# A state-space block and a mixture of experts in one kernel: five weight splits moved ahead of the first slots, and the second block's front begun five slots later

## The chip, the cores and the metric

The kernel runs on one NeuronCore of a Trainium2 chip. It takes float32 inputs and gives float32 outputs. The metric is the device time of one execution in microseconds; the time of a kernel is the median of its runs. All engines named here belong to that one core: TensorE (PE in the profile, with its weight loads as PEld), VectorE (DVE), ScalarE (ACT), GpSimd (POOL), and SyncE (SP), which only issues DMAs here. ScalarE's queue issues a few DMAs at the start and the end.

## The reference: what is computed

The input `u` has 16 batches of 512 tokens with 128 features. Each batch passes through two residual halves, both with a layer norm before and after:

```python
x = x + layernorm(state_space(layernorm(x)))      # Bu = x B^T; convolution with 64 complex modes; y = h C^T + D x
x = x + layernorm(experts(layernorm(x)))
```

The convolution kernel is `exp(t * log(eig))`, with eigenvalues on the unit circle that are worked out from `a_params`. The second half is a dense mixture of 8 experts: every token goes through every expert.

```python
h   = silu(x @ w_gate[e]) * (x @ w_up[e])          # 128 -> 512
out = sum over e of (h @ w_down[e]) * cw[:, e]     # 512 -> 128
cw  = softmax(x @ w_router) * softmax((x @ w_gating) / 0.1), normalised over e
```

## The kernel before

**Blocks and slots.** A block is one batch: 512 tokens. The expert half of block b is cut into 32 slots, one for each of 8 experts and 4 quarters of the 512 hidden features, so slot n has b = n // 32, e = n // 4 % 8, and there are 512 slots. In a slot, `up` (L554) makes g and uu, 128 hidden features by 512 tokens each; `gate` (L569) multiplies silu(g) and uu; `down` (L589) adds the slot's share to the expert's output d four slots later (`LAG`).

**Three matmuls for one.** A float32 product is made of float32r parts: each operand has a high part (a cast) and a low part (what the cast lost), and `mm3` (L337) issues high by high (L338), low weight by high (L339) and high weight by low (L340). A full slot is thus 9 matmuls of 128x512. The parts of the hidden h are `hi` (L580, ScalarE) and `lo` (L586, on VectorE, or on POOL where the planner's list `lo_pool` says so). The 24 weight matrices (3 for each expert: gate, up, down, in that order, numbered k = 3e + j) are split too: a cast on ScalarE (L110) and a subtraction on POOL (L115). The first `AHEAD` = 3 weights are split before slot 0 by `rest` (L679): TensorE multiplies by the identity and subtracts the high part by a negated identity, each of these in float32 with two passes, and ScalarE writes the result (L684). The others are split in the slots, one at a time (L837 to L839).

**Engines take their instructions in the order in which the program issues them.** The order is written out by hand in the loop over slots (L807 to L846), and a small planner decides where the rest goes. In slot n the loop issues: `hi` of slot n-1; g, uu and silu (`sg`, L564) of slot n; `down` of slot n-4; then, every fourth slot, `combine` (L596), which multiplies a finished d by the token weights `cwb` of its expert (L601 for the first expert of a block, L606 for the others) and adds it up; then one weight split; then `steps`; then `lo` of slot n-1; then the gate of slot n. For `combine` of expert e of block b that is slot 32b + 4e + 9.

**The planner.** `chain(b)` (L615) is a generator: layer norm, state space and second layer norm of block b (`front`, L346), then `route(b)` (L408), which makes the token weights. Each `yield` gives the slots to wait and the time it needs on VectorE, ScalarE and POOL. `steps` (L794) runs those that are due and fit into `SLOT` + a margin; a chain with `hurry` 1 may take two steps in a slot and waits a slot less. Block 1's chain begins in slot 0 with hurry 1 (L821), the others at max(4, 32b - 67). `back(b)` (L467) is the last layer norm of a finished block: a transpose on VectorE (`ob`, L473), four DMA writes (`sco`, L476), a DMA back (`ot`, L481), then statistics.

**From the logits to `cwb`.** `route` makes the logits on TensorE (`lg`, L415), the powers on POOL (`ez`, L433, eight instructions; block 0 uses ScalarE's exponential instead), sums and quotients on VectorE (L436 to L446), then the transpose `cwT` (L451). SP writes `cwT` to DRAM in four DMAs (`scw`, L454) and reads it back for two experts at a time, broadcast to all partitions (`cwb`, L462, 512 KB each). SP issues its DMAs in order, each after its own waits.

**Before slot 0.** Block 0's state space runs in a hand-ordered stretch (L641 to L773) with two halves of 256 tokens. `yp` (L675, L698) is its output, `residual` (L726) makes x2 and its statistics, `rstd` (L497) the scale on POOL (L505), `norm` (L513) the normalised xn, TensorE transposes it (L752), ScalarE writes the high part xh and the plain copy (L755, L756), VectorE the low part xl (L757). `keep_warm` (L734) issues 9 and 4 matmuls whose result nobody reads.

**Buffers that matter.** g has two PSUM banks, uu three, d two; `sg` two tiles in SBUF, `hi` and `lo` five each. The first `OWN` = 8 weights are loaded into tiles of `hi` and `lo`, the later ones into five tiles of their own.

Of the kernel before, what the change touches and what calls it, by code (L numbers as in the profile page):

```python
# [11 lines left out]
F32 = mybir.dt.float32  # L12
# [7 lines left out]
P = 128  # L20
T = 512
NT = T // P
# [4 lines left out]
NF = F // P  # L27
LAG = 4
LEAD = 67
OWN = 8  # L30
WARM = 9, 4, 0
AHEAD = 3
LN_EPS = 1e-5


# [12 lines left out]
def sandwich(ctx, tc, x, a_params, B_w, C_w, Dv, w_router, w_gating, w_gate, w_up, w_down, sines, out):  # L48
# [31 lines left out]
            nc.sync.dma_start(out=xts[b][:, k], in_=x[b].rearrange("(c p) d -> p c d", p=P)[:, k])  # L80


    spare = [hp.tile([P, F], F32R, name=f"spare{i}", tag="lo", bufs=LAG + 1).bitcast(F32) for i in range(2)]

# [49 lines left out]
    dbc = const.tile([P, D], F32, name="dbc")  # L136
    for k in range(AHEAD, OWN):
        load_w(k)
        if k == 4 and NB > 1:
            load_x(1)  # L140
            nc.sync.dma_start(out=dbc, in_=Dv.partition_broadcast(P))

# [25 lines left out]
    def bank(pl, tag, name):  # L168
        return pl.tile([P, T], F32, name=name, tag=tag)
# [176 lines left out]
    def front(b):  # L346
# [58 lines left out]
        vec.tensor_tensor(xl, xT, xh.bitcast(F32), ALU.subtract)  # L405
        blocks[b] = dict(xh=xh, xl=xl, x2=x2, xT=xT)

    def route(b):  # L408

        G2 = NT * 2  # L410
        xT = blocks[b]["xT"]
        yield 1, 0, 0, 0, "f"
        lg = ps_f.tile([P, G2, E], F32, name=f"lg{b}", tag="f")
        for c in range(NT):
            pe.matmul(  # L415
                lg[:, 2 * c : 2 * c + 2], xT[:, P * c : P * c + P], wrg.rearrange("d g e -> d (g e)"),
                start=True, stop=True,
            )
        yield 1, 0.4, 0, 0
        bc = lambda t, n: t.unsqueeze(2).broadcast_to([P, n, E])  # L420
        mx = small.tile([P, G2], F32, name="mx", bufs=2)
        vec.tensor_reduce(mx, lg, AX.X, ALU.max)
        ez = small.tile([P, G2, E], F32, name="ez", bufs=2)
        vec.tensor_tensor(ez, lg, bc(mx, G2), ALU.subtract)
        own[0] = False
        if b == 0:
            e4 = ez.rearrange("p (c g) e -> p c g e", g=2)
            act.activation(e4[:, :, 0], e4[:, :, 0], AF.Exp)
            act.activation(e4[:, :, 1], e4[:, :, 1], AF.Exp, scale=10.0)
        else:  # L430
            for i in range(G2):
                yield 1, 0, 0, 1.62
                gp.tensor_tensor(ez[:, i], bases.rearrange("p c g e -> p (c g) e")[:, i], ez[:, i], ALU.pow)  # L433
        yield 2, 0.65, 0, 0
        sm = small.tile([P, G2], F32, name="sm", bufs=2)
        vec.tensor_reduce(sm, ez, AX.X, ALU.add)  # L436
        vec.reciprocal(sm, sm)
        vec.tensor_tensor(ez, ez, bc(sm, G2), ALU.mult)
        yield 1, 0.75, 0, 0
        pr = ez.rearrange("p (c g) e -> p c g e", g=2)  # L440
        cw0 = small.tile([P, NT, E], F32, name="cw0", bufs=2)
        vec.tensor_tensor(cw0, pr[:, :, 0], pr[:, :, 1], ALU.mult)
        cs = small.tile([P, NT], F32, name="cs", bufs=2)
        vec.tensor_reduce(cs, cw0, AX.X, ALU.add)
        vec.tensor_scalar(cs, cs, 1e-9, None, ALU.add)
        vec.reciprocal(cs, cs)  # L446
        yield max(1, 32 * b - 8 - now[0]), 0.45, 0, 0
        cwt = cwp[b % 2]
        vec.tensor_tensor(cwt[:, :, 0:E], cw0, bc(cs, NT), ALU.mult)
        cwT = small.tile([P, NT, 32], F32, name="cwT", bufs=2)  # L450
        vec.transpose(cwT, cwt)  # L451
        scw = dram.tile([E, 4, P], F32, name=f"scw{b}", tag="scw")
        for c in range(4):
            nc.sync.dma_start(  # L454
                out=scw.rearrange("e q (c i) -> e q c i", i=32)[:, :, c], in_=cwT[32 * c : 32 * c + E]
            )
        cwb = []
        blocks[b]["cwb"] = cwb
        for i in range(4):
            yield max(1, 32 * b + 8 * i + 2 - now[0]), 0, 0, 0  # L460
            t = fe.tile([P, 2, T], F32, name=f"cwb{b}_{i}", tag="cwb", bufs=3)
            nc.sync.dma_start(  # L462
                out=t, in_=scw[2 * i : 2 * i + 2].rearrange("e q m -> e (q m)").partition_broadcast(P)
            )
            cwb.append(t)
# [47 lines left out]
    def norm(outs, views, rs, nm, shared):  # L513
        act.activation(outs[0], views[0], AF.Identity, scale=rs[:, 0:1], bias=nm[:, 0:1])
        if shared:
            vec.tensor_scalar(outs[1], views[1], rs[:, 1:2], nm[:, 1:2], ALU.mult, ALU.add)
        else:
            act.activation(outs[1], views[1], AF.Identity, scale=rs[:, 1:2], bias=nm[:, 1:2])

    def halves(t):  # L520
        return [[t[:, 2 * h], t[:, 2 * h + 1]] for h in range(2)]
# [110 lines left out]
    def turn(k):  # L632
        for _ in range(k):
            next(rot, None)
# [3 lines left out]
    def stat(c, view):  # L638
        vec.bn_stats(s6s[c // 2][:, c % 2], view)
# [39 lines left out]
    def rest(k, pl, tag):  # L679
        hi, lo = parts(k)  # L680
        ps = bank(pl, tag, f"rest{k}")
        pe.matmul(ps, ident, raw[k], start=True, stop=False)
        pe.matmul(ps, negid[:, 0], hi.bitcast(F32), start=False, stop=True)
        return lambda: act.copy(lo, ps)  # L684
# [10 lines left out]
    def state(c):  # L695
        k = quarter[c]
        vec.tensor_tensor(vm[:, k], v[:, k], tre[:, k], ALU.mult)
        pe.matmul(yps[c], vm[:, k], cT, start=False, stop=True)  # L698

    vec.tensor_tensor(v[:, left], bus[0], tre[:, left], ALU.mult)  # L700
    turn(2)
    scan(left, 0.0)
    turn(2)
    state(0)
    state(1)
    turn(2)
    vec.tensor_tensor(v[:, right], bus[1], tre[:, right], ALU.mult)
    lo0 = rest(0, ps_u, "u")
    lo0()
    scan(right, v[:, 2 * P - 1 : 2 * P])  # L710
    stat(0, yps[0])
    stat(1, yps[1])
    state(2)
    state(3)
    rest(1, ps_g, "g")()
    r0 = rstd(s6s[0])
    stat(2, yps[2])
    stat(3, yps[3])
    r1 = rstd(s6s[1])
    rest(2, ps_f, "f")()  # L720

# [5 lines left out]
            vec.scalar_tensor_tensor(x2[:, c], yps[c], rs[:, i : i + 1], xt[:, c], ALU.mult, ALU.add)  # L729
            stat(c, x2[:, c])  # L730

    warm = bank(ps_g, "g", "warm")

    def keep_warm(k):  # L734
        for _ in range(k):
            pe.matmul(warm, W[0, 0][0][:, :P], W[0, 0][0], start=True, stop=True)

    keep_warm(WARM[0])
    residual(0, r0[1])
    q0 = rstd(s6s[0])  # L740
    residual(1, r1[1])
# [3 lines left out]
    xh = fe.tile([D, T], F32R, name="xh0", tag="xh", bufs=2)  # L745
    xl = fe.tile([D, T], F32R, name="xl0", tag="xl", bufs=2)
    xT = work("ft_x0")
    for h, q in enumerate((q0, q1)):
        norm(halves(xn)[h], halves(x2)[h], q[1], shift(*q), True)
        ps = bank(ps_u, "u", f"xT0{h}")[:, : 2 * P]  # L750
        for i in range(2):
            pe.transpose(ps[:, P * i : P * i + P], xn[:, 2 * h + i], ident)  # L752
        keep_warm(WARM[1 + h])
        k = slice(2 * P * h, 2 * P * h + 2 * P)
        act.copy(xh[:, k], ps)  # L755
        act.copy(xT[:, k], ps)  # L756
        vec.tensor_tensor(xl[:, k], ps, xh[:, k].bitcast(F32), ALU.subtract)  # L757
    for h, r in enumerate((r0, r1)):
        vec.scalar_tensor_tensor(x2m[:, 2 * h : 2 * h + 2], r[0][:, :, 0], -1.0, r[1], ALU.mult, ALU.mult)
    blocks[0] = dict(xh=xh, xl=xl, x2=x2, xT=xT, x2m=x2m)  # L760
    first_route = route(0)

    def first():
# [43 lines left out]
    for n in range(total + LAG):  # L807
        b, s = divmod(n, 32)
        now[0] = n
        busy = [max(0.0, t - SLOT) for t in busy]  # L810
        if n < total:
            take((0.6, 1.0, 0), (9, 9, 9))
        if 0 <= n - 1 < total:
            take((0, 0, 1.23) if lo_pool[n - 1] else (0.6, 0, 0), (9, 9, 9))
            split_hi(n - 1)
        if n < total:
            up(n, *[first] * (n == 0))
        if n == 0:
            begin(n, 0, first_route, 1, routed)
            if NB > 1:  # L820
                begin(n, 1, chain(1), 1)  # L821
        if n == 3:
            act.copy(bT[0], bT32)
            gp.tensor_tensor(bT[1], bT32, bT[0].bitcast(F32), ALU.subtract)
        for i in range(NB):
            if i > 1 and n == max(4, 32 * i - LEAD):
                begin(n, i, chain(i))
        m = n - LAG
        if 0 <= m < total:
            down(m)  # L830
        m = n - LAG - (2 if n < total else n == total)
        if m >= 0 and m % 4 == 3:
            take((0.6, 0, 1.23), (9, 9, 9))
            combine(m // 32, m // 4 % 8)
            if m % 32 == 31 and m // 32 in accs:
                begin(n, m // 32 + 0.5, back(m // 32, accs.pop(m // 32)))
        if nsplit < 3 * E and n < total and n % 4 < 3:  # L837
            take((0, 0.5, 1.23), (9, 9, 9))
            split_next(1)  # L839
        if n < total:  # L840
            steps(n)
        if 0 <= n - 1 < total:
            split_lo(n - 1)
        if n < total:
            lo_pool[n] = busy[2] < busy[0] and n < total - 3
            gate(n)  # L846


# [25 lines left out]
```

## Time and profile before

| what | value |
|---|---|
| median of 3 runs | 1156.02 us (1155.92 to 1157.78) |
| the profiled execution | 1155.96 us |
| its span in the profile | 1154.1 us |
| TensorE busy | 1131.5 us (98%) |
| VectorE, ScalarE, POOL busy | 922.9, 698.1, 745.6 us |
| DMA, share of 16 engines (main queue) | 20.0% |
| first matmul of slot 0 | at 26.41 us |
| last d matmul ends | at 1146.1 us |

Times in the profile count from the start of the span. A row of a timeline shows the start, the duration, the engine with line and operation, what it writes and reads (without buffer numbers), shapes and count; in brackets, how long the engine sat idle before it and what ended that. Matmuls overlap in a pipeline: a matmul of 128x512 is shown with 0.39 us, while the next one starts 0.23 us after it. In a table of windows the columns are the stretch, its length, busy time and count of PE, PEld, DVE, ACT and POOL, then the granted TensorE clock as a share of full speed, the busy share of the DMA engines and GB/s. SPq rows are DMA issues: their duration is that of the issue, not of the transfer.

### The profile page before, as it was taken

Reading aid. Unit: us, or ns where it says so; the run is one execution under the profiler, and the core shown is the slowest. Engines: PE = TensorE matmul, PEld = TensorE weight load, DVE = VectorE, ACT = ScalarE, POOL = GpSimd, SP = SyncE. Lnnn points to the kernel's source line nnn. Section 1 sums busy time; section 2 is a strip of 40 time slices with the busy share of each in tenths; the row PEclk is TensorE's granted clock in tenths of the full one; section 3 lists DMA queues with packets and bytes.
Section 4 is the critical chain, followed back from the end, with each engine's and each line's share of the span. In section 5 each row is a group of like instructions: output and inputs, shape, how many; then the busy total and the mean of one; then the engine's idle time right before and its main releaser. Section 6 shows DMA issues by size and latency. Waiting matters only on the chain.

```text
span 1154.1 us, 16183 instructions
## 1 busy us (share of the span) xinstructions
PE 1131.5 (98%) x4978; PEld 913.3 (79%) x4978; DVE 922.9 (80%) x2101; ACT 698.1 (60%) x1348; POOL 745.6 (65%) x570
## 2 busy tenths in 40 slices
PE   6899999999999999999999999999999999999997
PEld 4678788888888888888888888888888888888885
DVE  6888888887878878787887878888787887868666
ACT  3766656656566655656566565655657566565564
POOL 1679576776757766585866748577585856647442
PEclk9999999999999999999999999999999999999999
DMA  4140312203122131302212130130302202111120
GB/s 152 50 149 4 93 55 56 92 29 92 47 65 64 38 96 43 92 28 74 73 38 83 38 109 29 56 90 30 92 29 81 66 19 74 47 56 28 31 71 10
DMA packets 65894, 71.23 MB, mean 62 GB/s; under 512 B 8624, under 2 KB 50320, under 8 KB 65808
## 3 DMA queue, kind: packets, MB, share of 16 engines
q1 hardware_dynamic: 65392, 70.04, 20.0%
q8 instruction: 39, 0.64, 0.2%
q14 instruction: 47, 0.39, 0.1%
q10 hardware_dynamic: 416, 0.16, 0.1%
HBM read 54.98 MB, written 15.20 MB: 61 GB/s over the span
## 4 chain that ended last, share of the span: by engine, by line
PE 90%; DVE 4%; POOL 3%; issue 2%; ACT 0%; DMA 0%; DVEq 0%; POOLq 0%
PE g L338 10%; PE d L338 10%; PE g L340 10%; PE d L339 10%; PE uu L338 10%; PE d L340 10%; PE uu L340 10%; PE g L339 10%; PE uu L339 9%; PE yp L387 1%; POOL ez L433 1%; PE lg L415 1%; DVE x L302 0%; POOL acc L609 0%; DVE lo L586 0%
## 5 line engine op out<-in xcount | busy, mean ns | idle before, releaser
L586 POOL TENSOR_TENSOR lo<-hh,hi 128x512 fp32r<-128x512 f32 x196 | 261.9, 1336 | 155.1 <-ACT hi L580 155.0
L580 ACT CAST hi<-uu 128x512 fp32r<-128x512 f32 x316 | 185.4, 587 | 244.4 <-DVE uu L575 235.9
L564 ACT ACTIVATE sg<-g 128x512 f32<-128x512 f32 x512 | 306.7, 599 | 17.5 <-PE g L340 11.7
L575 DVE TENSOR_TENSOR uu<-sg,uu 128x512 f32<-128x512 f32 x316 | 218.7, 692 | 93.9 <-ACT sg L564 83.3
L586 DVE TENSOR_TENSOR lo<-uu,hi 128x512 fp32r<-128x512 f32 x316 | 216.9, 687 | 95.9 <-ACT hi L580 93.2
L609 POOL TENSOR_TENSOR acc<-acc,ct 128x512 f32<-128x512 f32 x109 | 142.4, 1306 | 138.9 <-DVE ct L606 89.7
L580 ACT CAST hi<-hh 128x512 fp32r<-128x512 f32 x196 | 121.6, 621 | 162.5 <-DVE hh L575 160.7
L338 PE MATMUL g<-xh,wgh 128*128 128x512 f32 x512 | 206.8, 404 | 2.4 <-ACT sg L564 1.8
L338 PE MATMUL uu<-xh,wuh 128*128 128x512 f32 x512 | 203.9, 398 | 4.3 <-DVE lo L586 4.3
L339 PE MATMUL d<-hi,wdl 128*128 128x512 f32 x512 | 203.3, 397 | 0.0
L340 PE MATMUL g<-xl,wgh 128*128 128x512 f32 x512 | 203.1, 397 | 0.0
L338 PE MATMUL d<-hi,wdh 128*128 128x512 f32 x512 | 203.0, 396 | 0.0
L340 PE MATMUL uu<-xl,wuh 128*128 128x512 f32 x512 | 201.4, 393 | 0.0
L340 PE MATMUL d<-lo,wdh 128*128 128x512 f32 x512 | 201.1, 393 | 0.0
L339 PE MATMUL g<-xh,wgl 128*128 128x512 f32 x512 | 200.8, 392 | 0.0
L339 PE MATMUL uu<-xh,wul 128*128 128x512 f32 x512 | 198.6, 388 | 0.0
L433 POOL TENSOR_TENSOR ez<-bases,ez 128x8 f32<-128x8 f32 x120 | 195.7, 1650 | 0.0
L575 DVE TENSOR_TENSOR hh<-sg,uu 128x512 f32<-128x512 f32 x196 | 133.5, 681 | 12.5 <-ACT sg L564 5.1
L338 PEld LDWEIGHTS g<-xh,wgh 128*128 128x128 f32 x512 | 96.1, 188 | 27.7 <-ACT sg L564 5.2
L338 PEld LDWEIGHTS uu<-xh,wuh 128*128 128x128 f32 x512 | 95.9, 187 | 27.8 <-DVE lo L586 6.0
L339 PEld LDWEIGHTS uu<-xh,wul 128*128 128x128 f32 x512 | 96.4, 188 | 23.8 <-POOL wul L115 0.2
L340 PEld LDWEIGHTS d<-lo,wdh 128*128 128x128 f32 x512 | 96.8, 189 | 22.9
(172 smaller groups left out, 1336.8 us busy)
## 6 DMA issues: line engine op xcount, KB each, us to landing
cwb<-scw SPq DMA_DIRECT2D x64, 512.0 KB
xt<-in_L_attn_u_dram SPq DMA_DIRECT2D x15, 256.0 KB
sco<-ob SPq DMA_DIRECT2D x60, 64.0 KB
ot<-sco SPq DMA_DIRECT2D x15, 256.0 KB
out_dram<-x SPq DMA_DIRECT2D x15, 256.0 KB
scr_u<-blk_u SPq DMA_DIRECT2D x52, 64.0 KB
ft_u<-scr_u SPq DMA_DIRECT2D x13, 256.0 KB
scr_x<-blk_x SPq DMA_DIRECT2D x52, 64.0 KB
```

Of the source, the lines that this page charges most:

```text
L338: pe.matmul(ps, w[0][:, cs], mh, start=first, stop=False)
L339: pe.matmul(ps, w[1][:, cs], mh, start=False, stop=False)
L340: pe.matmul(ps, w[0][:, cs], ml, start=False, stop=last)
L387: pe.matmul(yp[:, c], v[:, P * c : P * c + P], cT, start=True, stop=True)
L415: pe.matmul(lg[:, 2 * c : 2 * c + 2], xT[:, P * c : P * c + P], wrg.rearrange("d g e -> d (g e)"), start=True, stop=True,)
L433: gp.tensor_tensor(ez[:, i], bases.rearrange("p c g e -> p (c g) e")[:, i], ez[:, i], ALU.pow)
L564: act.activation(s, g, AF.Silu)
L575: vec.tensor_tensor(h, s, u, ALU.mult)
L580: act.copy(hi, pend[n])
L586: (gp if lo_pool[n] else vec).tensor_tensor(lo, h, hi.bitcast(F32), ALU.subtract)
L609: add = lambda: eng.tensor_tensor(acc, acc, t, ALU.add)
```

## The change

What it does, in the order of the program:

- `AHEAD` goes from 3 to 5: weights 3 and 4 are also split before slot 0 by `rest`, on TensorE and ScalarE. The matmuls of `rest` stand earlier in TensorE's order, and the ScalarE writes of the low parts are gathered behind the statistics of yp.
- `OWN` goes from 8 to 7; weights 3 and 4 are loaded ahead of the router weights, block 1's input after weight 6. A third spare tile takes a `lo` buffer.
- The warm matmuls go. All four quarters of xn are made on VectorE from mean and scale; the two xl follow the two halves' copies; two of four logit chunks are issued before slot 0's g, the other two after it.
- Weight splits in the slots begin at slot 4. In slots 0 to 3 the low part of h is on VectorE.
- Block 0's route is handed to the planner one slot later; block 1's chain begins in slot 5, not in slot 0; the parts of B are made in slot 4.
- In a slot the times of sum and split are booked first, then `steps` runs, and only then `combine` and the split are issued. Before, both were issued ahead of `steps`.

```diff
-OWN = 8
-WARM = 9, 4, 0
-AHEAD = 3
+OWN = 7
+AHEAD = 5
...
-        if k == 4 and NB > 1:
+        if k == OWN - 1 and NB > 1:
             load_x(1)
...
+    def score(lg, xT, cs):
+        for c in cs:
             pe.matmul(
                 lg[:, 2 * c : 2 * c + 2], xT[:, P * c : P * c + P], wrg.rearrange("d g e -> d (g e)"),
                 start=True, stop=True,
             )
...
     vec.tensor_tensor(v[:, left], bus[0], tre[:, left], ALU.mult)
+    lo = [rest(0, ps_u, "u")]
...
     state(1)
+    lo.append(rest(1, ps_f, "f"))
...
-    lo0 = rest(0, ps_u, "u")
-    lo0()
     scan(right, v[:, 2 * P - 1 : 2 * P])
+    lo.append(rest(2, ps_g, "g"))
...
     state(3)
-    rest(1, ps_g, "g")()
+    lo.append(rest(3, ps_g, "g"))
...
     r1 = rstd(s6s[1])
-    rest(2, ps_f, "f")()
+    lo[0]()
+    lo[1]()
+    lo.append(rest(4, ps_f, "f"))
+    for f in lo[2:]:
+        f()
...
-    keep_warm(WARM[0])
...
+            vec.tensor_scalar(xn[:, c], x2[:, c], mv[:, i, 0:1], rs[:, i : i + 1], ALU.subtract, ALU.mult)
+            pe.transpose(ps[:, P * i : P * i + P], xn[:, c], ident)
+        act.copy(xh[:, (left, right)[h]], ps)
+        act.copy(xT[:, (left, right)[h]], ps)
+    for h, k in enumerate((left, right)):
+        vec.tensor_tensor(xl[:, k], xps[h], xh[:, k].bitcast(F32), ALU.subtract)
+    score(lg, xT, (0, 1))
...
         if n == 0:
-            begin(n, 0, first_route, 1, routed)
-            if NB > 1:
-                begin(n, 1, chain(1), 1)
-        if n == 3:
+            begin(n + 1, 0, first_route, 1, routed)
+        if n == 5 and NB > 1:
+            begin(n, 1, chain(1), 1)
+        if n == 4:
             act.copy(bT[0], bT32)
...
+        adds = m >= 0 and m % 4 == 3
+        splits = nsplit < 3 * E and 4 <= n < total and n % 4 < 3
+        if adds:
             take((0.6, 0, 1.23), (9, 9, 9))
+        if splits:
+            take((0, 0.5, 1.23), (9, 9, 9))
+        if n < total:
+            steps(n)
+        if adds:
             combine(m // 32, m // 4 % 8)
             if m % 32 == 31 and m // 32 in accs:
                 begin(n, m // 32 + 0.5, back(m // 32, accs.pop(m // 32)))
-        if nsplit < 3 * E and n < total and n % 4 < 3:
-            take((0, 0.5, 1.23), (9, 9, 9))
+        if splits:
             split_next(1)
-        if n < total:
-            steps(n)
...
-            lo_pool[n] = busy[2] < busy[0] and n < total - 3
+            lo_pool[n] = busy[2] < busy[0] and 4 <= n < total - 3
```

More of the change, by code (lines that the diff above doesn't have):

```diff
@@ L80, in load_x @@
             nc.sync.dma_start(out=xts[b][:, k], in_=x[b].rearrange("(c p) d -> p c d", p=P)[:, k])
-    spare = [hp.tile([P, F], F32R, name=f"spare{i}", tag="lo", bufs=LAG + 1).bitcast(F32) for i in range(2)]
+    spare = [hp.tile([P, F], F32R, name=f"spare{i}", tag="lo", bufs=LAG + 1).bitcast(F32) for i in range(3)]
     raw = {}
@@ L406, in front, with logits @@
         blocks[b] = dict(xh=xh, xl=xl, x2=x2, xT=xT)
+    def logits(b):
+        return ps_f.tile([P, NT * 2, E], F32, name=f"lg{b}", tag="f")
+    def score(lg, xT, cs):
+        for c in cs:
+            pe.matmul(
+                lg[:, 2 * c : 2 * c + 2], xT[:, P * c : P * c + P], wrg.rearrange("d g e -> d (g e)"),
+                start=True, stop=True,
+            )
     def route(b):
@@ L412, in route @@
         yield 1, 0, 0, 0, "f"
[L413 to L418, printed above, removed]
+        if b > 0:
+            lg = logits(b)
+            score(lg, xT, range(NT))
+        else:
+            lg = blocks[0]["lg"]
+            score(lg, xT, (2, 3))
         yield 1, 0.4, 0, 0
@@ L730, in residual @@
             stat(c, x2[:, c])
[L732 to L736, printed above, removed]
-    keep_warm(WARM[0])
     residual(0, r0[1])
@@ L747, in sandwich @@
     xT = work("ft_x0")
-    for h, q in enumerate((q0, q1)):
-        norm(halves(xn)[h], halves(x2)[h], q[1], shift(*q), True)
+    xps = []
+    lg = logits(0)
+    for h, (mv, rs) in enumerate((q0, q1)):
         ps = bank(ps_u, "u", f"xT0{h}")[:, : 2 * P]
+        xps.append(ps)
         for i in range(2):
[L752 to L760, printed above, removed]
+            c = 2 * h + i
+            vec.tensor_scalar(xn[:, c], x2[:, c], mv[:, i, 0:1], rs[:, i : i + 1], ALU.subtract, ALU.mult)
[5 more added lines that the diff above has]
+    score(lg, xT, (0, 1))
+    for h, (mv, rs) in enumerate((r0, r1)):
+        vec.scalar_tensor_tensor(x2m[:, 2 * h : 2 * h + 2], mv[:, :, 0], -1.0, rs, ALU.mult, ALU.mult)
+    blocks[0] = dict(xh=xh, xl=xl, x2=x2, xT=xT, x2m=x2m, lg=lg)
     first_route = route(0)
@@ L831, in sandwich @@
         m = n - LAG - (2 if n < total else n == total)
-        if m >= 0 and m % 4 == 3:
+        adds = m >= 0 and m % 4 == 3
+        splits = nsplit < 3 * E and 4 <= n < total and n % 4 < 3
+        if adds:
             take((0.6, 0, 1.23), (9, 9, 9))
+        if splits:
[3 more added lines that the diff above has]
+        if adds:
             combine(m // 32, m // 4 % 8)
```

## The prediction

> **What bounds the kernel now.** I read the page first (busy shares, the chain that ended last), then TensorE's timeline with its idle times, then the windows where it idles, then the queues of the engines named there.
>
> ```profile
> PE 1131.5 (98%) x4978; PEld 913.3 (79%) x4978; DVE 922.9 (80%) x2101; ACT 698.1 (60%) x1348; POOL 745.6 (65%) x570
> ...
> PE 90%; DVE 4%; POOL 3%; issue 2%; ACT 0%; DMA 0%; DVEq 0%; POOLq 0%
> ```
>
> TensorE is 98% busy and 90% of the chain. So only three things can move the time: when slot 0 starts, TensorE's holes, and work added to it. The timeline of TensorE shows each hole in brackets:
>
> ```profile
> 31.31 0.50 PE L338 MATMUL g<-xh,wgh 128*128 128x512 f32 x1 [0.72 <-ACT sg L564]
> ...
> 37.88 0.50 PE L338 MATMUL uu<-xh,wuh 128*128 128x512 f32 x1 [1.88 <-DVE lo L586]
> ...
> 75.05 0.79 PE L338 MATMUL uu<-xh,wuh 128*128 128x512 f32 x1 [2.17 <-DVE lo L586]
> ...
> 123.86 0.50 PE L338 MATMUL g<-xh,wgh 128*128 128x512 f32 x1 [0.71 <-ACT sg L564]
> ```
>
> After 123.86 no hole follows until the tail. I call the start of a slot's first L338 g matmul T(n). A full slot lasts 2.09 (T8 46.38, T9 48.47); T0 is 26.41, T37 116.72, T40 123.86. The slot lengths beyond 2.09 and beyond other TensorE work sum, from slot 9 on, to 6.0: 0.43 in slot 13, 0.47 in 18, 3.77 in 19, 0.15 in 20, 0.3 in 29, 0.88 in 39. Slot 19 is so dear because a hole also costs clock (third number from the right):
>
> ```profile
> 74.00:76.00 2.00, 0.95 (x2) 0.83 (x3) 2.00 (x7) 0.38 (x1) 0.00 (x0) 0.67 0.38 132
> 76.00:78.00 2.00, 2.00 (x6) 1.54 (x5) 1.57 (x8) 2.00 (x5) 0.68 (x1) 0.50 1.02 322
> ```
>
> From 75.05 to 77.78 matmuls start every 0.43 instead of 0.23: some 1.5 us lost after the 2.17 us hole.
>
> **How late VectorE may be.** `hi(n)` on ScalarE stands ahead of `sg(n+1)`, and the two g banks make `g(n+3)` wait for `sg(n+1)`. So if the gate of slot n (L575) ends later than T(n)+5.0 (6.27 for three slots, less 0.62 for hi and 0.59 for sg), TensorE stops. In slot 40 it ended at 128.40, T40+4.5: the reserve is under a microsecond.
>
> **Change, part 1: the head.** Lows of weights 3 and 4 move to TensorE: 8 passes at 0.43 (L682, L683 before 21.4 us) or 0.23 once warm. rest 0 to 2 now stand ahead of the last two yp products: these issued at 16.69; now after yp 0 and 1 (15.3) come rest 1 and 2, 8 passes, so 17.2 warm or 18.8 cold. VectorE's chain to x2 shifts with them by 0.5 to 2.1. Given back: all four xn on VectorE in a row, no warm matmuls ahead of the transposes, no half-by-half wait (xl 24.44, second xn 24.97, transposes 25.52). The new chain: yp done at 18.7 (nearer the cold end, since the clock now rises only at 21.4), +5.0 as now to the last scale rsh on POOL (17.1 to 22.10), +0.6 for the last two xn, +0.5 for their transposes, +0.4 for xh: g0 at 25.3, against 26.41. Ends: 24.0 and 26.2. **-1.1.** Half of the logits (4 of 8 passes) stand ahead of g0, so first sg follows g0 by 3.6 instead of 4.25 (30.66-26.41): **-0.6.** Removing 13 warm matmuls (2.63 and 1.17 us of TensorE at 20.87 and 23.48; the transposes waited for the first nine) leaves TensorE idle from about 20.5 to 23.7. The trace: 1.88 us of idling (36.0) left the clock at 1.00, 2.17 us (72.9) halved it. The Trainium skill ("TensorE: Matmul & The Clock Gate", Part 1: The HAM clock gate) says that about 3.4 us of idling halves it and as much work restores it. By the row slot 0 runs half-clocked, +0.6; by the page 3.2 us may just pass, 0. I take **+0.3**.
>
> Slots 1 to 3 lose three weight casts on ScalarE (0.61 each at 31.15, 33.03, 34.86), but these lay in ScalarE's wait for the gate: sg 0.60, gate 0.69, hi 0.62, overlapped, give 1.85 a slot (sg at 30.66, 32.54, 34.37) with or without them. Worth 0; without that cover 0.6 a slot. The lows of h in slots 0 to 3 move from POOL (1.27 to 1.30) to VectorE (0.69), which has 0.5 a slot to spare there beside a gate and a low in 1.85; the loads of weights 3 and 4 go ahead of the router's on SP, a microsecond earlier than now, and are wanted at 17: both worth 0. POOL's weight lows and block 1's steps leave slots 0 to 4, so the 2.28 hole of slot 4 (uu after lo, behind L286 at 1.22 beside POOL) goes. What is late next: weight 7, the up weight of expert 2, is now split in slot 6, not 5, and POOL has wdl1, wgl2, lo4, rs, then wul2 in line. From the cast of weight 5 (first sg+9.9): 1.3, wait to +11.8, 1.3, 1.3, 1.0, 1.3: wul2 ends at +16.7, but slot 8 wants it at +14.4. A hole of 2.35 there, 0.7 in slots 6 and 7 (small route steps before lo2), 0.6 after nm in slots 9 to 12. T9 comes at first sg+17.95, against 17.81 now, and block 1's transposes (0.44) are then still to come: **+1.2** with the 0.6. Head in all: -1.1-0.6+0.3+1.2 = **-0.2** (-2 to +2).
>
> **Part 2: block 1 begun five slots later, front ahead of the sum.** x21's four instructions (L302) move from slot 17, with a ct (0.68), to slot 22 without it. They took 3.19 beside POOL; POOL is as busy there (acc, two weight lows at 1.3). 6.0 goes, **+1.6** comes (0 to 4.4, what they cost now).
>
> The route's last step moves too, and with it its four scw writes and the cwb load on SP. Now:
>
> ```profile
> 119.30 0.31 DVE L451 STREAM_TRANSPOSE cwT<-cwp 128x128 f32<-128x128 f32 x1
> 119.54 2.52 DVE L302 SCALAR_TENSOR_TENSOR x<-du,rs,xt 128x128 f32<-128x128 f32 x2
> 121.98 0.67 DVE L575 TENSOR_TENSOR hh<-sg,uu 128x512 f32<-128x512 f32 x1
> ...
> 123.83 0.70 DVE L575 TENSOR_TENSOR uu<-sg,uu 128x512 f32<-128x512 f32 x1 [0.16 <-ACT sg L564]
> ...
> 125.80 0.68 DVE L575 TENSOR_TENSOR hh<-sg,uu 128x512 f32<-128x512 f32 x1
> ...
> 127.71 0.69 DVE L575 TENSOR_TENSOR hh<-sg,uu 128x512 f32<-128x512 f32 x1 [0.78 <-issue]
> 128.32 0.68 DVE L601 TENSOR_TENSOR acc<-d,cwb 128x512 f32<-128x512 f32 x1
> ```
>
> Four gates lie between cwT and the first product that needs cwb. On SP, the same moment:
>
> ```profile
> 119.64 2.84 SPq L454 DMA_DIRECT2D scw<-cwT  x4
> 123.73 0.33 SPq L462 DMA_DIRECT2D cwb<-scw  x1
> ...
> 125.17 2.07 SPq L476 DMA_DIRECT2D sco<-ob  x4
> 129.70 0.34 SPq L481 DMA_DIRECT2D ot<-sco  x1
> ```
>
> Block 0's load, issued at 43.13, ends by the traffic (last number, GB/s) at about 46.4:
>
> ```profile
> 44.00:45.00 1.00, 1.00 (x6) 0.77 (x6) 0.71 (x6) 1.00 (x3) 1.00 (x2) 1.00 0.75 254
> 45.00:46.00 1.00, 1.00 (x6) 0.83 (x5) 0.98 (x2) 1.00 (x3) 0.98 (x1) 1.00 0.76 258
> 46.00:47.00 1.00, 1.00 (x6) 0.82 (x5) 0.82 (x2) 1.00 (x3) 0.99 (x1) 1.00 0.05 21
> ```
>
> So cwT to landing: 119.61 to 123.73 is 4.1, plus 3.3: **7.4**. The built program's order on VectorE, with what each waits for, now reads at the two places:
>
> ```
> cwT_1567<-cwp1 [DVE]; x22 [ACT] x2; acc1<-d32,cwb1_0 [DMA]; hh41<-sg41,uu41 [PE,ACT]
> cwT_2395<-cwp0 [DVE]; hh72<-sg72,uu72 [PE,ACT,POOL]; acc2<-d64,cwb2_0 [DMA]; uu73<-sg73 [PE,ACT]
> ```
>
> In block 1 no gate lies between cwT and acc1: both are built in slot 41, front step first, sum behind it. cwT ended at T37+2.9; moved, it ends at T41+2.9 to 4.6 (the POOL powers L433 now end behind one more acc); 3.8. Then acc1 starts at 3.8+7.4 = 11.2, gate 41 ends at 12.5 (0.6+0.69), hi 13.1, sg42 13.7, and g44, due at 6.27, starts then: a hole of **7.4** (6 to 9). Behind the waiting acc1 stand gate 41 and every later gate; hi41, sg42 and TensorE wait for those.
>
> Block 2 meets it again: cwT in slot 72, one gate, acc2 in slot 73 ahead of gate 73, so g76 waits. On SP the four scw2 now stand behind sco1 (4), ot1, scr_u4 (4), ft_u4. From ob1's end: 2.0, 1.4 to 2.46 until ot, 0.4, 1.8, 1.4 to 2.15, 0.4, 2.83, 1.24, landing 3.3: 14.6 to 16.7, then 2.5 as above: 18.1. ob1 ends at about T71+2.0; g76, due at T71+10.45, starts at 20.1: **9.7** (7 to 12). Blocks from 3 on have 25 or more VectorE instructions between cwT and product; block 5 has 12 of them now and shows no hole.
>
> Clock: after such holes the row gives +1.5 each, the skill's rule (half rate for 3.4 us) 1.7. I take the row: **+3.0**; by the rule the sum is 0.4 more.
>
> **Sum.** -0.2-6.0+1.6+7.4+9.7+3.0 = +15.5, on the profiled execution's 1155.96 (span 1154.1 plus 1.86 around it; the median is 1156.02): **1171.5 us**.
>
> **Rivals.** (a) Only the first wait costs, because SP sends block 2's scw writes at once and the load lands inside TensorE's three ready slots: -9.7-1.5, 1160.3. For: with SP free the load would land 7.4 after cwT, and a gate stands between; against: sco1 to ft_u4 are ten issues that queue ahead on SP. 0.16. (b) Each wait leaves VectorE (80% busy) a backlog that it works off at 1.85 a slot, and cwb's second load, issued right behind, shares the engines: +3 each, 1177.5. 0.10. (c) The other sign: the waits hide, for instance because gates run early enough that TensorE has over three slots ready. Then -0.2-6.0+1.6 = -4.6, 1151.4. It decides where both waits with their clock together cost under 4.6; against it gate 40's reserve of 0.5. 0.08. (d) Gains and waits cancel within 0.2% (2.3 us, about what a measurement of this kernel can tell from no change): 0.04.
>
> **Numbers.** The likeliest case (0.62) spans 1164 to 1179. Range 1160 to 1179: rival (a) included, (c) and part of (b) left out. Slower 0.88, same 0.04, faster 0.08.
>
> **What would show it.** Right: two TensorE holes near slots 44 and 76 of 6 us or more, VectorE idle before the first acc of blocks 1 and 2 for a DMA on cwb, clock 0.50 after each; first sg near 29; a smaller hole at slot 8 released by POOL wul. Wrong: no wait at these products, or slot 0 past 27.

## The result, and the profile after

| | kernel before | changed kernel |
|---|---|---|
| median | 1156.3 us (1155.92 to 1157.78) | 1176.82 us (1176.01 to 1178.97) |
| the profiled execution, and its span | 1155.96 us, 1154.1 | 1176.01 us, 1174.2 |
| start of slots 0, 9, 40, 80 | 26.41, 48.47, 123.86, 210.60 | 25.62, 47.21, 124.91, 231.28 |

The ratio is 1.0178 (1.0160 to 1.0196): slower by some 20.5 us, and 5.3 above the forecast. The row of slot starts (the first L337 g matmul of each slot in TensorE's timeline) shows where: the changed kernel enters slot 9 earlier by 1.26 us, loses 2.3 us up to slot 40 (and is 1.05 behind there), and loses 19.6 more between slots 40 and 80. After slot 80 the two run alike, to within 0.6 us.

From the page of the changed kernel, busy time by engine and the chain that ended last:

```profile
PE 1137.7 (97%) x4973; PEld 917.2 (78%) x4973; DVE 915.3 (78%) x2102; ACT 701.1 (60%) x1348; POOL 738.6 (63%) x567
...
PE 84%; DVE 2%; DMA 1%; ACT 1%; issue 0%; SPq 0%; DVEq 0%; ACTq 0%
```

VectorE and POOL have less to do than before, and TensorE's share of the chain fell from 90% to 84%, with a DMA in the list that was at 0%. The large holes in TensorE's timeline (start, duration, what; in brackets the idle time and what ended it):

```profile
45.96 0.50 PE L338 MATMUL uu<-xh,wul 128*128 128x512 f32 x1 [2.00 <-POOL wul L114]
...
86.64 0.48 PE L337 MATMUL uu<-xh,wuh 128*128 128x512 f32 x1 [2.25 <-DVE lo L595]
...
140.10 0.79 PE L337 MATMUL g<-xh,wgh 128*128 128x512 f32 x1 [6.67 <-ACT sg L573]
...
219.44 0.80 PE L337 MATMUL g<-xh,wgh 128*128 128x512 f32 x1 [8.51 <-ACT sg L573]
```

These lie in slots 8, 24, and ahead of g44 and g76. sg is only the last link. VectorE's timeline at the first sums of blocks 1 and 2 (in the kernel before, block 1's stood at 128.32 and waited for no load):

```profile
129.23 0.31 DVE L460 STREAM_TRANSPOSE cwT<-cwp 128x128 f32<-128x128 f32 x1
129.46 0.57 DVE L301 SCALAR_TENSOR_TENSOR x<-du,rs,xt 128x128 f32<-128x128 f32 x2
137.61 0.69 DVE L610 TENSOR_TENSOR acc<-d,cwb 128x512 f32<-128x512 f32 x1 [7.58 <-DMA cwb<-scw]
138.22 0.68 DVE L584 TENSOR_TENSOR hh<-sg,uu 128x512 f32<-128x512 f32 x1
...
216.98 0.69 DVE L610 TENSOR_TENSOR acc<-d,cwb 128x512 f32<-128x512 f32 x1 [10.54 <-DMA cwb<-scw]
```

The first sums of blocks 1 and 2 stop VectorE for 7.58 and 10.54 us, with the slot's gate behind them. The queue of SP says what the load was late for:

```profile
129.57 2.83 SPq L463 DMA_DIRECT2D scw<-cwT  x4
133.56 0.81 SPq L471 DMA_DIRECT2D cwb<-scw  x2
...
204.83 0.34 SPq L490 DMA_DIRECT2D ot<-sco  x1
205.21 1.91 SPq L327 DMA_DIRECT2D scr_u<-blk_u  x4
208.66 0.34 SPq L332 DMA_DIRECT2D ft_u<-scr_u  x1
209.04 2.83 SPq L463 DMA_DIRECT2D scw<-cwT  x4
213.03 1.29 SPq L471 DMA_DIRECT2D cwb<-scw  x3
```

In block 1 SP was free: cwT ended at 129.54, the writes began at once, and the sum started 8.07 us after cwT. In block 2 cwT ended at 204.95, but its writes were issued at 209.04, behind `scr_u` and `ft_u`. A few windows show the clock behind each hole (stretch, length, PE, PEld, DVE, ACT, POOL, then the granted clock):

```profile
140.00:142.00 2.00, 1.90 (x5) 1.52 (x6) 1.08 (x3) 1.67 (x4) 2.00 (x2) 0.50 0.67 223
142.00:144.00 2.00, 2.00 (x8) 1.62 (x7) 1.73 (x5) 1.09 (x2) 1.37 (x2) 0.75 0.47 170
...
221.00:223.00 2.00, 2.00 (x6) 1.55 (x5) 1.59 (x3) 1.69 (x4) 1.22 (x1) 0.50 0.00 0
223.00:225.00 2.00, 2.00 (x6) 1.59 (x5) 2.00 (x5) 0.88 (x2) 0.00 (x0) 0.52 0.00 0
```

To compare runs I count, for TensorE's matmuls of g, uu and d, what lies beyond 0.23 us between one start and the next: as "hole", or, where the spacing is 0.43, as "half clock".

| us, hole + half clock | slots 9 to 39 | slots 40 to 51 | slots 72 to 81 |
|---|---|---|---|
| before | 5.4 + 1.0 | 0.1 + 0 | 0 + 0 |
| changed | 6.1 + 1.6 | 7.3 + 1.0 | 9.2 + 2.1 |

### The profile page after: what moved, and what is told of

Its sections match the earlier page's. It is cut to its first block, busy times and chain, and to the rows that moved or that the text cites. A ratio compares the mean times of both kernels' runs of the same rounds, so it can differ in the third digit from the quotient of the medians.

```text
span 1174.2 us, 16187 instructions
## 1 busy us (share of the span) xinstructions
PE 1137.7 (97%) x4973; PEld 917.2 (78%) x4973; DVE 915.3 (78%) x2102; ACT 701.1 (60%) x1348; POOL 738.6 (63%) x567
## 4 chain that ended last, share of the span: by engine, by line
PE 84%; DVE 2%; DMA 1%; ACT 1%; issue 0%; SPq 0%; DVEq 0%; ACTq 0%
PE g L337 9%; PE g L339 9%; PE d L337 9%; PE d L338 9%; PE uu L337 9%; PE d L339 9%; PE uu L339 9%; PE g L338 9%; PE uu L338 9%; PE yp L386 1%; PE lg L412 1%; DVE uu L584 1%; ACT hi L589 0%; DMA cwb<-scw 0%; DVE lo L595 0%
## 5 line engine op out<-in xcount | busy, mean ns | idle before, releaser
L595 POOL TENSOR_TENSOR lo<-hh,hi 128x512 fp32r<-128x512 f32 x195 | 259.3, 1331 | 151.8 <-ACT hi L589 151.7
L337 PE MATMUL g<-xh,wgh 128*128 128x512 f32 x512 | 207.7, 406 | 15.5 <-ACT sg L573 15.4
L337 PE MATMUL uu<-xh,wuh 128*128 128x512 f32 x512 | 204.8, 400 | 2.4 <-DVE lo L595 2.2
L337 PE MATMUL d<-hi,wdh 128*128 128x512 f32 x512 | 203.3, 397 | 0.0
L337 PEld LDWEIGHTS g<-xh,wgh 128*128 128x128 f32 x512 | 96.6, 189 | 40.3 <-ACT sg L573 18.0
L337 PEld LDWEIGHTS uu<-xh,wuh 128*128 128x128 f32 x512 | 96.6, 189 | 25.6 <-issue 2.7
L339 PEld LDWEIGHTS g<-xl,wgh 128*128 128x128 f32 x512 | 96.9, 189 | 23.7 <-DVE xl L767 0.4
```

Of the source, the lines that this page charges most:

```text
L337: pe.matmul(ps, w[0][:, cs], mh, start=first, stop=False)
L339: pe.matmul(ps, w[0][:, cs], ml, start=False, stop=last)
L595: (gp if lo_pool[n] else vec).tensor_tensor(lo, h, hi.bitcast(F32), ALU.subtract)
```

## Experiments

Times stand beside the median of the kernel before in the same group of runs: 1156.73 for the first four, 1156.46 for the next four, 1156.05 for the last four. Ratios are to the kernel before, with their 95% intervals. The expectations count the runs as they were made: the first has block 1's wait taken away, the second both waits, the third the start in slot 0, the fourth that start with splits from slot 3.

### The two waits, taken away one after the other

```diff
         if e == 0:
             accs[b] = fe.tile([P, T], F32, name=f"acc{b}", tag="acc")
+            if b in (1,):              # second run: (1, 2)
+                cw = blocks[b - 1]["cwb"][3][:, 0]
             vec.tensor_tensor(accs[b], ps, cw, ALU.mult)
```

> The changed kernel with one edit: the first sum of block 1 takes the weights of an expert of block 0, loaded long before, in place of the first half of cwb1_0, so it waits for no load (the tokens of block 1 get wrong weights for expert 0; every instruction stays). Theory (the waits are the loss, and each is paid by itself): the 6.8 us hole ahead of g44 and its half clock of 1.5 go, the hole ahead of g76 (8.7) stays: 1176.8 - 8.3 = 1168.5. Rival 1 (the loss is in the first 30 slots, and the wait covers a backlog of VectorE that comes out behind it): 1174 or more. Rival 2 (block 2's wait follows from block 1's, because its steps were pushed back by the stop): both go, 1157.5.

> As the run before, and the first sum of block 2 takes an expert's weights of block 1 likewise (wrong weights for expert 0 in both blocks; every instruction stays). Theory: both holes and both stretches at half clock go, 6.8 + 1.5 + 8.7 + 2.3 = 19.3: 1157.5, so that the rest of the change is worth about nothing against before (1156.3). Rival 1 (the loss is in the first 30 slots): 1170 or more. Rival 2 (the parts beside the waits gain what rival (c) of the prediction said, 4.6): 1151.5.

Measured: 1168.77 us (1.0105, 1.0090 to 1.0120) without the first wait, 1157.81 (1.0009, 1.0000 to 1.0017) without both. So taking away the first gives 8.0 and then the second 11.0; 19.0 of the 20.5 us. They are not quite independent: without the first wait, TensorE idled 9.66 ahead of g76, not 8.51. Without its wait block 1's product follows cwT at once. VectorE, second run:

```profile
129.32 0.31 DVE L460 STREAM_TRANSPOSE cwT<-cwp 128x128 f32<-128x128 f32 x1
129.56 0.57 DVE L301 SCALAR_TENSOR_TENSOR x<-du,rs,xt 128x128 f32<-128x128 f32 x2
130.05 0.68 DVE L612 TENSOR_TENSOR acc<-d,cwb 128x512 f32<-128x512 f32 x1
130.65 0.68 DVE L584 TENSOR_TENSOR hh<-sg,uu 128x512 f32<-128x512 f32 x1
```

Rival 1 of both runs (the loss is in the first 30 slots) falls, and so does rival 2 of the first (both waits go together). Rival 2 of the second falls too: all that is not these waits came to +1.1 (0 to 2.0 by the interval), where the forecast had -4.6.

### Which part brings the waits

The second part of the change alone, on the kernel before:

```diff
         if n == 0:
             begin(n, 0, first_route, 1, routed)
-            if NB > 1:
-                begin(n, 1, chain(1), 1)
+        if n == 5 and NB > 1:
+            begin(n, 1, chain(1), 1)
...
+        if n < total:
+            steps(n)             # ahead of combine and split_next, no longer behind
```

> The kernel before with the second part of the change alone: block 1's chain begins in slot 5, and steps are issued ahead of sum and split. The head, the splits from slot 0 and the lows of h on POOL stay as before. In the program no gate stands between cwT and the first product in block 1, and one in block 2, as in the changed kernel. Theory (this part alone brings both waits): both holes appear, 1156.3 + 19.3 = 1175.6, within 3. Rival (the waits need the head's later splits too): 1165 or less.

Measured: 1175.39 us (1.0164, 1.0150 to 1.0178). TensorE idles ahead of g44 and g76 as in the changed kernel:

```profile
139.95 0.80 PE L338 MATMUL g<-xh,wgh 128*128 128x512 f32 x1 [6.45 <-ACT sg L564]
...
219.62 0.79 PE L338 MATMUL g<-xh,wgh 128*128 128x512 f32 x1 [8.35 <-ACT sg L564]
```

The late start and the order are enough; the head isn't needed. A late start with the old order was not run. Nor is the late start needed for waits to appear: with the start in slot 0, the later splits bring them too, as the next runs show.

### The start in slot 0 again, and what SP does to it

The changed kernel with the start undone, and then also with block 0's and 1's last layer norm a slot later:

```diff
-        if n == 5 and NB > 1:
+        if n == 0 and NB > 1:
             begin(n, 1, chain(1), 1)
...
-                begin(n, m // 32 + 0.5, back(...))
+                begin(n + 1 * (m // 32 in (0, 1)), m // 32 + 0.5, back(...))   # second run only
```

> The changed kernel with block 1's chain begun in slot 0 again; all else of the change stays. In the program two gates then stand between cwT and the first product in both blocks (the changed kernel has none in block 1 and one in block 2, the kernel before four and five). Theory (each gate between is a slot of 2.09 that the load may take, of about 7.4): block 1's hole falls from 6.8 by 4.2 to 2.6, block 2's from 8.7 by 2.1 to 6.6, clock as before or a little less: 1176.8 - 6.3 = 1170.5, within 2. Rival (the start in slot 5 is the whole cause of the waits): both holes go, 1157 to 1159.

> The changed kernel with block 1's chain from slot 0, as in the third run, and one more edit: the last layer norm of blocks 0 and 1 begins one slot later. The gates between cwT and the first product stay two and two; on SP the four scw writes of block 1 then stand ahead of the four sco writes and ot of block 0, and in block 2 the scw writes stand ahead of sco and ot, but the cwb load still behind them. Theory (in the third run the two slots won were eaten on SP: cwT ended at 127.5, its scw writes were issued at 130.76, behind sco and ot): block 1's hole falls from 6.8 by 3.3 to 3.5, block 2's by 0 to 1: 1174.8 - 3.8 = 1171, within 1.5. Rival (the queue on SP does not matter, the load is late for its transfer): 1174 or more.

Measured: 1174.76 us (1.0157, 1.0142 to 1.0173), a miss by 4, and 1168.96 (1.0103, 1.0088 to 1.0118). SP in the first of the two, where cwT ended at 127.49 (T41-1.7, against T41+2.5 in the changed kernel):

```profile
127.09 1.78 SPq L485 DMA_DIRECT2D sco<-ob  x4
130.33 0.34 SPq L490 DMA_DIRECT2D ot<-sco  x1
130.76 2.83 SPq L463 DMA_DIRECT2D scw<-cwT  x4
135.25 0.35 SPq L471 DMA_DIRECT2D cwb<-scw  x1
```

and in the second, where it ended at 125.24:

```profile
125.27 2.84 SPq L463 DMA_DIRECT2D scw<-cwT  x4
129.35 0.33 SPq L471 DMA_DIRECT2D cwb<-scw  x1
129.78 2.25 SPq L485 DMA_DIRECT2D sco<-ob  x4
```

The 4.2 us that two more gates gave were taken back between cwT and the sum, which now lie 12.3 us apart and not 8.07: the writes stood 3.3 us behind four `sco` and an `ot` that waits for them, and the writes and the load took 0.9 longer. TensorE still idled 6.63 ahead of g44. With the writes first it idled 1.64. The second run also fell by more than forecast (5.8, not 3.8), since cwT itself came 0.6 earlier against its slot and block 2's hole shrank from 6.4 to 4.8.

### The splits one place earlier

```diff
-        splits = nsplit < 3 * E and 4 <= n < total and n % 4 < 3
+        splits = nsplit < 3 * E and 3 <= n < total and (n == 3 or n % 4 < 3)
```

alone on the changed kernel, then with the start in slot 0, then this last version with the old order of a slot (`combine` and `split_next` ahead of `steps`):

> The changed kernel with one edit: the weight splits in the slots begin in slot 3, not 4, so every weight is split one place earlier; block 1 still begins in slot 5. In the program the gates between cwT and the first product stay as in the changed kernel (none in block 1, one in block 2). Theory (the split that comes a place too late is a loss of its own beside the waits): the hole at slot 8 (2.1, released by POOL's low part of weight 7, and 1.5 of half clock behind it) goes, and the one at slot 28 (1.3, likewise) too; both waits stay: 1176.8 - 4.9 = 1172, within 1.5. Rival 1 (slot 8's loss comes out elsewhere, because POOL is as busy): 1175 or more. Rival 2 (the early splits alone take the waits away, as in the run with both edits): 1157 or less.

> As the run before, and the weight splits in the slots begin in slot 3, not 4, so that every weight is split one place earlier. In the program four gates stand between cwT and the first product in block 1 and five in block 2, as in the kernel before. Theory: both waits go (19.3), and weight 7 is split in slot 5 again, so the hole at slot 8 (2.1, with 1.5 of half clock behind it) goes too; block 1's steps are back in slots 0 to 4, worth up to 2.5 there: 1153.5 to 1157. Rival (the new head and the steps ahead of the sum cost by themselves): 1160 or more.

> The fourth run's kernel (block 1 from slot 0, splits from slot 3) with the order in a slot put back: sum and split ahead of the steps, as in the kernel before. Theory (with the load early enough, steps ahead of the sum is worth little: the steps of one slot are some 0.7 of VectorE ahead of or behind a 0.6 product): 1150.5 to 1155.5, the same as the fourth run's 1152.9 within 0.2%. Rival (the new order is what makes that version faster than the kernel before): 1156 or more.

Measured: alone 1177.11 us (1.0169, 1.0152 to 1.0186), no gain. With the start in slot 0: **1152.86 us (0.9966, 0.9956 to 0.9977), faster than both kernels**. With the old order as well: 1153.0 (0.9968, 0.9955 to 0.9981), the same.

In the first, slot 8's hole is gone and comes out one slot later, as its rival 1 said:

```profile
48.61 0.79 PE L337 MATMUL uu<-xh,wuh 128*128 128x512 f32 x1 [2.08 <-DVE lo L595]
```

Ahead of that lo, VectorE's nm (L285) had waited 1.53 for POOL's rs and then took 1.25 beside POOL's next weight low. The second shows that start and splits must go together: either alone leaves it at 1174.8 or 1177.1. The pair brings cwT back to four and five gates ahead of the products, as before, and no sum waits for a load. Block 1's on VectorE:

```profile
116.64 0.31 DVE L460 STREAM_TRANSPOSE cwT<-cwp 128x128 f32<-128x128 f32 x1
...
126.23 0.67 DVE L610 TENSOR_TENSOR acc<-d,cwb 128x512 f32<-128x512 f32 x1
```

What it keeps of the change is the first slots: slot 9 starts at 46.02, against 48.47 in the kernel before. The order within a slot, half of what the forecast called part 2, is worth nothing there.

### The start in slot 5 with more haste

```diff
         if n == 5 and NB > 1:
-            begin(n, 1, chain(1), 1)
+            begin(n, 1, chain(1), 2)
...
-                begin(n, i, chain(i))
+                begin(n, i, chain(i), int(i <= 2))
```

(with splits from slot 3)

> The changed kernel with splits from slot 3 and block 1 begun in slot 5, but with more haste in the planner: block 1's chain may take three steps in a slot and waits two slots less, block 2's may take two and waits one less. In the program five gates then stand between cwT and the first product in block 1 and 17 in block 2. Theory (only the lateness of cwT costs, not the start in slot 5): both waits go: 1152 to 1157. Rival (pressed steps make VectorE late in many slots, which is why the start in slot 5 is dear): 1159 or more.

Measured: 1162.3 us (1.0045, 1.0030 to 1.0060); the theory missed by 5 or more. No sum waits for cwb any more, but slots 9 to 39 hold 9.5 of holes and half clock together, and slots 40 to 51 another 2.8. In them uu stops seven times for lo, by 0.4 to 1.1 each, and besides TensorE idles 1.99 ahead of yp, which waits for VectorE's ez. So late token weights are the dear part of a late start, not the only one. Which of the pressed steps makes VectorE late was not taken apart.

### The stretch in slot 22

The run without both waits, and block 1's x21 products dealt over two slots:

```diff
             if c % 2 == 0:
-                yield 1, 0.52, 0, 0
+                yield 1 + (c == 2 and now[0] < 30), 0.52, 0, 0
             vec.scalar_tensor_tensor(outs[c], views[c], rs[:, c : c + 1], adds[c], ALU.mult, ALU.add)
```

> The second run's kernel (the changed kernel, first sums of blocks 1 and 2 without a wait for the load) with block 1's four x21 products dealt over two slots, two and two, with a gate and the low part of h between; the later steps of block 1 stay in their slots. Theory (the four took 4.82 us in one stretch in slot 22, some 1.35 each beside POOL in place of 0.31, and that made lo and g late for a hole of 2.2 at slot 24 and half clock of 0.8 to 1.2 behind it; this is the term that the forecast put at 1.6): the hole goes, 1157.8 - 2.5 = 1155.3, within 1. Rival (the hole has another cause, or the stretch costs the same in two pieces): 1157 or more.

VectorE in slot 22 of the changed kernel, and then the same products in this run:

```profile
80.48 0.68 DVE L584 TENSOR_TENSOR uu<-sg,uu 128x512 f32<-128x512 f32 x1
81.08 4.82 DVE L301 SCALAR_TENSOR_TENSOR x<-du,rs,xt 128x128 f32<-128x128 f32 x4
85.81 0.68 DVE L595 TENSOR_TENSOR lo<-uu,hi 128x512 fp32r<-128x512 f32 x1
```

```profile
81.08 2.24 DVE L301 SCALAR_TENSOR_TENSOR x<-du,rs,xt 128x128 f32<-128x128 f32 x2
83.25 0.68 DVE L595 TENSOR_TENSOR lo<-uu,hi 128x512 fp32r<-128x512 f32 x1
83.85 0.68 DVE L584 TENSOR_TENSOR uu<-sg,uu 128x512 f32<-128x512 f32 x1
84.44 1.71 DVE L301 SCALAR_TENSOR_TENSOR x<-du,rs,xt 128x128 f32<-128x128 f32 x2
```

Measured: 1156.62 us (0.9998, 0.9990 to 1.0007), 1.2 below the run that it is made from, half of what the theory said; the intervals of the two runs overlap, so the median alone does not show the gain. In the traces the hole of slot 24 went (2.6 to 0.2; slot 25 starts 2.5 earlier), so it did come from this stretch. But slot 28 now waits for POOL's low part of expert 7's up weight (hole 1.8, against 0.2), and by slot 30 the lead is 1.2.

In the version at 1152.86 the same four products meet POOL work only at their end (a weight low that starts at 69.67) and take a quarter of the time:

```profile
68.89 1.13 DVE L301 SCALAR_TENSOR_TENSOR x<-du,rs,xt 128x128 f32<-128x128 f32 x4
```

### Two parts of the head

On the version at 1152.86: the low parts of h in slots 0 to 3 back on POOL, and five matmuls that nobody reads ahead of the transposes.

```diff
-            lo_pool[n] = busy[2] < busy[0] and 4 <= n < total - 3
+            lo_pool[n] = busy[2] < busy[0] and 0 <= n < total - 3      # first run only
...
+    warm = bank(ps_d, "d", "warm")                                     # second run only
+    for _ in range(5):
+        pe.matmul(warm, W[0, 0][0][:, :P], W[0, 0][0], start=True, stop=True)
```

> The fourth run's kernel (block 1 from slot 0, splits from slot 3) with the low parts of h in slots 0 to 3 back on POOL where the planner puts them there. Theory (they lie beside ScalarE's pace in these slots, either way): the same within 0.2%, 1150.5 to 1155.2. Rival (VectorE's early slots are where that version gains): 1156 or more.

> The fourth run's kernel with five matmuls that nobody reads ahead of the transposes of xn, so that TensorE idles some 1.2 us less before slot 0. Theory (the half clock from 27 to 30 goes, but slots 0 to 3 go at the pace of ScalarE and VectorE, whose first sg waits for the powers of the logits until 29.6): granted clock near 1.00 from 26 to 30, the time as before within 1: 1152 to 1154. Rival (the half clock at the start costs its full length): 1151 or less.

Measured: 1152.86 us (0.9970, 0.9960 to 0.9979) and 1153.1 (0.9971, 0.9961 to 0.9981): both the same as without. In the first the planner puts two of the four lows, those of slots 0 and 2, on POOL. With the warm matmuls the clock reads 1.00 from 20 to 32 us, slot 1 starts at 27.56 and not 28.65, and slot 5 at 35.78 and not 36.24; by slot 8 the lead is 0.5 us, and the median shows nothing of it: slot 40 starts at 121.57, against 120.91 without. The old order and the lows on POOL enter slot 9 earlier too, at 45.28 and 44.95 against 46.02, and yet start slot 40 at 120.92 and 120.94. So in this version up to a microsecond won in the first slots is gone by slot 40; what takes it back was not tested.

## Why the prediction was right, and where its sum was off

**The two waits** were the mechanism, at the places named, and held. Step by step, block 1: cwT at T41+2.5 (forecast 3.8), 8.07 to the sum's start (7.4), 2.49 from there to g44 (2.5): a hole of 6.8 (7.4). Block 2: g76 at T71+19.1 (20.1): a hole of 8.7 (9.7). (The forecast's terms for block 2's way through SP add up to 14.8 to 16.6, not 14.6 to 16.7; the middle that it used is the same.) Without the waits the time falls by 8.0 and 11.0. Rival (a) fell: block 2's writes did queue on SP, behind `scr_u` and `ft_u` at least, for 4.1 us. Rivals (c) and (d) fell with the measured time: both waits stand in the trace, and by the second run the rest gains nothing to set against them.

**The clock** behind them: 1.0 and 2.1, together 3.1 (3.0 by the row, 3.4 by the rule). The sum cannot choose between the two here.

**The head.** g0 at 25.62 (25.3), first sg at 29.54 (some 28.9), a hole of 2.3 at slot 8 (2.35), released by POOL's wul as forecast. Slot 9 came 1.26 earlier, and -1.1 - 0.6 + 0.3 + 0.14 is -1.26 too, with a little luck: first sg came 1.1 earlier, not 1.4, and from there to slot 9 it took 17.67, not 17.95. Two steps had the wrong reason. The forecast had the `rest` passes at 0.43 because TensorE was cold, and 0.23 once warm (see below). And it had TensorE idle from 20.5 to 23.7: the passes went on to 22.85, the longest hole from there to slot 0 is 0.79, and the clock fell to 0.50 all the same, from 27 to 30.

**The term that failed** is "6.0 goes, +1.6 comes", with 0.6 for slots 9 to 12: for slots 9 to 39 that leaves 2.2, and the trace has 7.6. x21 was expected to cost 1.6 out of 0 to 4.4. It cost 2.6, the hole in slot 24: the four products took 4.82 where the forecast carried over the 3.19 of the kernel before. And the hole at slot 8 was given no clock, though the forecast gave it to both large holes: 1.6 in slot 9. The third part was not seen at all: the weight that comes a place too late was followed once, for slot 8, while the same wait for POOL's weight lows comes back at slots 16 (0.4), 20 (0.9) and 28 (1.5, expert 7's up weight, split in slot 26 for slot 28). These are 1.0, 1.6 and 2.8 of the difference.

By slot starts, forecast and trace compare so: up to slot 9 -1.26 in both; from 9 to 40 -3.4 against +2.3; from 40 to 80 +20.1 against +19.6; behind slot 80 nothing against -0.6. Together that is about the 4.5 us by which the profiled execution is above 1171.5, and nearly all of it lies in slots 9 to 39.

**Rival (b)** named 1177.5, nearly the measured time, by a backlog of 3 us behind each wait. The backlog isn't there: behind g44 and g76 little more than the half clock remains, and the removal of both waits gave about their holes and their clock. The time came near (b)'s figure by the early slots instead.

## What to carry to other kernels

When a step is moved, follow its result to the first instruction that needs it in the built order of every engine, and count two things there: the instructions between (one slot of cover each), and what stands ahead on the queue that issues its DMA. A write to DRAM and a load back took 8 us here, four slots, and a consumer in an in-order queue passes that wait to everything behind it. An edit of a planner's due times is judged by where the built program puts the steps: here a split one place earlier and a start five slots earlier were each worth nothing or little, and together 24 us.

## What had not been expected of the hardware

**A float32 pass at full clock takes 0.43 us.** TensorE in the changed kernel before slot 0, two `rest` rows (two passes each), and the window that holds them:

```profile
19.25 1.02 PE L691 MATMUL rest<-raw,ident 128*128 128x512 f32 x2
20.11 1.02 PE L692 MATMUL rest<-wgh,negid 128*128 128x512 f32 x2
```

```profile
20.00:21.00 1.00, 1.00 (x4) 0.41 (x3) 0.96 (x4) 0.00 (x0) 0.70 (x1) 1.00 0.00 0
```

The rows are 0.86 apart and the granted clock is 1.00. The five weights split ahead of slot 0 (three of them already in the kernel before) thus cost 20 passes of 0.43 each at full clock; a float32r pass of that size takes 0.23.

**A hole of 2 us can halve the clock, not at once and not every time.** After slot 8's hole of 2.00, which ended at 45.96, the clock stayed at 1.00 for another 1.5 us and then fell:

```profile
46.00:47.00 1.00, 1.00 (x5) 0.83 (x6) 0.96 (x5) 0.84 (x2) 1.00 (x1) 1.00 0.07 18
47.00:48.00 1.00, 1.00 (x5) 0.81 (x4) 1.00 (x3) 0.00 (x0) 0.89 (x2) 0.71 0.77 234
48.00:49.00 1.00, 1.00 (x4) 0.81 (x3) 0.37 (x1) 0.59 (x2) 0.27 (x1) 0.50 0.03 10
```

After slot 24's hole of 2.25 in the same trace the clock stayed at 1.00. In the run without both waits, the same hole of 2.25 at the same place was followed by half clock. The two windows:

```profile
88.00:90.00 2.00, 2.00 (x10) 1.44 (x9) 1.80 (x8) 1.12 (x3) 0.37 (x1) 1.00 0.92 252
```

```profile
88.00:90.00 2.00, 2.00 (x6) 1.38 (x5) 1.80 (x8) 1.12 (x3) 0.31 (x1) 0.50 0.81 308
```

Holes of 3.02 in slot 24 of two other runs (the second part alone, and the splits one place earlier alone) left the clock at 1.00 as well. A hole of 1.64 (ahead of g44 in the run with SP's writes first) cost nothing in slots 40 to 51, while in the changed kernel the one of 6.67 cost 1.0 and that of 8.51 cost 2.1. So between 2.0 and 3.0 us the length of a hole did not settle whether it costs clock here; what does, these runs do not show. The Trainium skill ("TensorE: Matmul & The Clock Gate", Part 1: The HAM clock gate) speaks of about 3.4 us without work; by that, slots 8 and 24 would both have been free. That fits slot 24 in this trace, but slot 8 cost 1.6. The measurement decides.

**A VectorE product with two inputs in SBUF takes four times as long beside POOL.** x21's products (128x128 of float32, from du and xt) took 1.2 on average in slot 22, with POOL busy all through with the sum acc and weight lows at 1.3 each, and 0.3 in the version at 1152.86, where POOL was idle for most of it. The Trainium skill ("SBUF — State Buffer", SBUF: two separate sides) says that a VectorE instruction with two SBUF inputs and a GpSimd instruction that reads SBUF lock each other out for a whole instruction. The rows agree: gates and lows, with one input in PSUM, kept their 0.7 in the same slots. The forecast had taken over the 3.19 that the four took in the kernel before, with POOL less busy beside them; the planner books 0.52 for two.
